# A softmax shift whose blockwise maxima reach one row through a TensorE transposition instead of a VectorE transposition and ScalarE copies

## The chip, the cores and the metric

The kernel runs on one NeuronCore of a Trainium2 chip. The metric is device time in microseconds of one execution; lower is better. The engines are TensorE (PE; its weight loads are PEld), VectorE (DVE), ScalarE (ACT), GpSimd (POOL) and SyncE (SP), which here issues all DMAs. Each engine takes its instructions in the order in which they stand and waits on semaphores for the others.

## What is computed

A cross-attention block in float32: x is 8 x 256 x 512, ctx is 8 x 256 x 512, with 16 heads of 32 columns and an MLP of 2048.

```
x1  = layer_norm(x, ln1_w, ln1_b)
q, k, v = x1 @ q_w + q_b, ctx @ k_w + k_b, ctx @ v_w + v_b      # split into 16 heads of 32
scores  = where(mask, q @ k^T / sqrt(32), smallest float)
attn    = softmax(scores, axis=-1)
hidden  = (attn @ v) @ cproj_w + cproj_b + x
y       = gelu(layer_norm(hidden, ln2_w, ln2_b) @ fc_w + fc_b) @ proj_w + proj_b
out     = hidden + y
```

## The kernel before, in words

The batch is done in two groups of four (g = 0, 1). All products with a weight matrix (k, q, v, the output projection o, and the MLP's fc and pd) are Strassen-Winograd products: `quad` (L848) makes seven products P1 to P7 of half-size blocks into PSUM banks X, Y and W, and VectorE or ScalarE adds them up (`t1`, `c11`, `c22`, `c21`, `c12`). The MLP applies the scheme twice, one inside the other. The sums of weight blocks that it needs are made early (`fw`, `pw`, L1080) and kept in DRAM.

Attention runs in 32 units, each of four heads and one batch element (`scores`, L1009). A unit is named by group, head group and batch element, so 012 is group 0, head group 1, batch element 2. For a unit the steps are:

- `s`: 16 matmuls in which TensorE is split by rows, one head in each quarter; keys lie on the 128 partitions, in two chunks kc, queries along the free axis.
- `ev`: ScalarE brings the eight pieces to SBUF with the mask added, into two buffers `pr`, one for each pair of heads.
- `mx` (L1022): for each pair, one VectorE reduction that transposes blocks of 32 x 32 takes the maximum over 32 keys. Its 128 x 64 result holds, for both chunks, maxima over quarters of the keys.
- `mt` (L1026), `mc` (L1029), `fold` (L1030): the eight partial maxima of a query have to be brought together. VectorE transposes the 128 x 64 block in squares of 32; ScalarE copies partitions 32 to 63, 64 to 95 and 96 to 127 beside partitions 0 to 31, in three instructions; one VectorE reduction over eight values leaves 32 x 32 maxima.
- `md`, `mm`: the 4 KB go to DRAM and come back as one row, spread over all 128 partitions (512 KB).
- `less` (L1048): the row is subtracted, on GpSimd in two instructions or on VectorE in one; `exp` (ScalarE).
- `av` (L1057): TensorE split by columns makes the sums of the exponentials (`ones`) and the products with v; VectorE inverts and scales (`r`, `att`).

Nothing of this order is left to a scheduler. `PROGRAM` (L124) is a list of all operations, written out by hand or by a planner; each engine's instructions stand in the order in which their names appear there, and a letter behind the colon chooses the engine (V VectorE, A ScalarE, G GpSimd). `PLACES` (L355) gives each buffer its slot. PSUM has eight banks, named W0 to W2 and C0 to C4 in before; a buffer of kind W (products) or C (scores, `av`, transpositions) lies in a bank of its own kind unless the table says otherwise. The scores of a unit need four banks.

At the end, group 1's last product `pd14` leaves its fourth product (`pd14_V`) turned, four pairs of transpositions (`ps_o`, L1312) bring the rest into the same shape, and VectorE adds residual and products into `ot`. Three stores of `ot` end the kernel; before them SyncE issues the stores of `tq` (`so1`, L1344), which are cut into pieces of 128 bytes.

Of the kernel before, what the change touches and what calls it, by code (L numbers as in the profile page):

```python
# [10 lines left out]
F32 = mybir.dt.float32  # L11
# [5 lines left out]
P = 128  # L17
# [26 lines left out]
class Order:  # L44
# [49 lines left out]
    def run(self):  # L94
# [20 lines left out]
        for o in order:  # L115
            for b in o.bufs:
                if b.slot is None and b.name in where:
                    w = where[b.name]
                    b.home = w[0] if not w[0].isdigit() else b.kind
                    b.slot = int(w.lstrip("WC"))  # L120
# [11 lines left out]
fw0s2:V fw1_10_1 xt0_5 k0_0_P6 fw0i6_3:V xt0_4 k0_1_t1:V fw0i6_1:G cb fw0i5_1:G v0_1_P3 k0_0_t2:V kws4:G fw0i1_4:V
k0_1_P6 stats_x0_30 fw0i1_3:G fw1i1_1:V stats_x0_00 fw0i6_2:G k0_0_P5 fw1i1_3:V k0_1_t2:A xt0_7 v0_0_t2:V fw1i1_2:G
fw0_01_1 stats_x0_10 fw1i1_4:G fcd0_1_True aggr_x0_30 k0_1_P5 fw1i4_1:V qw01 aggr_x0_00 stats_x0_01 fw1i4_2:G
fw1_01_0 fw0i6_4:V fcd0_6_False stats_x0_11 k0_1_P7 k0_1_t3:A fw1_01_1 aggr_x0_01 fw0i7_3:V k0_0_t3:A eps_x0_0
fcd0_7_False stats_x0_31 pow_x0_0 qw00 aggr_x0_31 k0_1_P3 fw1i4_4:G k0_1_c22 fcd0_7_True fw0i5_2:G aggr_x0_11
fcd0_5_False nb_x0_0 k0_0_c11 fw0i5_4:G norm_x0_01:A v0_0_P5 aggr_x0_10 k0_1_c11 fw0i2_1:G norm_x0_00:A fw1i4_3:V
k0_1_c12:A fw0i2_2:V k0_0_P7 eps_x0_1 eps_x0_3 fw0i5_3:V stats_x0_20 pow_x0_3 stats_x0_21 pow_x0_1 k0_0_P3 nb_x0_3
nb_x0_1 fw0i2_3:V norm_x0_31:A aggr_x0_20 aggr_x0_21 eps_x0_2 fw0i2_4:V norm_x0_10:A pow_x0_2 k0_0_c22 fcd0_2_True
k0_1_P4 v0_0_t3:V fw1i2_1:G fcd1_4_True k0_0_c12:A fcd0_6_True norm_x0_11:A nb_x0_2 fw0s4:V kd0_0_11 k0_0_P4  # L140
fcd1_1_True vws3:V norm_x0_20:A fcd0_3_False fw1i2_2:V fcd0_5_True norm_x0_21:A qws1:V turn_x0_10 norm_x0_30:A
fw1i2_4:G k0_0_c21 turn_x0_00 x0_10:A turn_x0_20 turn_x0_30 x0_20:A v0_0_P3 x0_30:V qws3:G xt1_2 cb1_02 x0_00:V
v0_1_c12:A fw0i3_1:V turn_x0_31 fw1i2_3:V turn_x0_11 fw0i3_2:V x0_31:A turn_x0_21 fw1s1:V turn_x0_01 q0_0_P1
x0_01:A qws2:G v0_0_c12:V fcd1_5_False x0_21:A k0_1_c21 fcd1_2_True fw1i5_3:G cb1_20 x0_11:A q0_0_P2 cb1_03
q0_0_t1:A x0t1:V q0_1_P1 fw0i3_3:V q0_0_c11 x0t2:V s000 fw0i3_4:V x0t3:V q0_0_P6 ev000_11 ev000_31 fw1s3:V xt1_3
ev000_10 ev000_01 cb1_12 q0_0_P7 x0t4:V kd0_0_21 q0_0_t2:A fcd1_7_False q0_1_t1:A fw1s2:V ev000_21 ev000_00 q0_0_P5
mx000_0 fw1s4:G fcd1_6_False cb1_10 q0_1_P6 q0_0_t3:A ev000_30 q0_0_c22 ev000_20 stats_x1_10 fcd1_3_False q0_1_P2
fw1i3_3:V fw1i5_1:V q0_1_t2:V fw1i5_2:G mx000_1 q0_0_P4 fw1i6_1:G qws4:G q0_1_c11 q0_1_P5 q0_0_c21 fw1i5_4:V mt000
fw0i4_3:G fcd1_5_True mc000_3 mc000_2 s020 cb1_13 mc000_1 fw1i6_3:G fold000 cb1_00 fw1i7_1:V q0_0_P3 md000 ev020_30
fw0i4_1:V ev020_21 fw1i7_2:V cb1_23 ev020_00 fw0i4_2:G cb1_21 ev020_10 fw1i7_4:G ev020_20 cb1_01 q0_1_P7 ev020_01  # L150
cb1_11 fw1i3_1:G ev020_31 q0_0_c12:A mx020_1 fw1i6_2:G ev020_11 s002 fw1i3_2:G mm000 mx020_0 fw0i4_4:G v0_1_P7
fw1i7_3:G mt020 stats_x1_11 mc020_2 mc020_3 fw1i6_4:G q0_1_t3:V ev002_30 ev002_11 fw1i3_4:G aggr_x1_10 aggr_x1_11
v0_0_P7 mc020_1 q0_1_c22 ev002_01 ev002_00 fold020 ev002_10 eps_x1_1 md020 ev002_31 pow_x1_1 ev002_20 q0_1_P3
# [358 lines left out]
def tile_xattn_block(  # L512
# [43 lines left out]
    def tile_of(b):  # L556
        if b.t is None:
# [874 lines left out]
    W = {}  # L1432
# [66 lines left out]
```

## Time and profile before

| | |
|---|---|
| three runs | 662.99, 663.53 (median) and 665.47 us |
| span of the profiled execution, first to last instruction | 662.0 us |
| own time of the profiled execution, beyond its span | not recorded apart; the runs lie 1.0 to 3.5 us above the span |
| instructions | 11469 |
| granted TensorE clock, mean over the span | 1.000 |
| DMA | 144.84 MB, mean 219 GB/s |

The profile is of one execution. A group line gives the line of the code, the engine, the operation, what it writes and reads, the shapes and the count, then busy time in us and the mean ns of one, then the engine's idle time just before and what ended it. A timeline line gives start and duration in us. Matmuls are pipelined, so the duration of one is longer than the step to the next one's start; the step is what it costs TensorE when it has no wait. For a DMA the issuing engine's instruction is shown, not the transfer.

### The profile page before, as it was taken

How to read it: one execution, taken by the hardware profiler on the slowest of the kernel's cores; microseconds unless marked ns; L12 is line 12 of the kernel's file. 1: busy time of each engine (PE TensorE's matmuls, PEld its weight loads, DVE VectorE, ACT ScalarE, POOL GpSimd, SP SyncE). 2: the span in 40 equal slices, each digit the busy share in tenths (PEclk: the TensorE clock that was granted, in tenths of full speed). 3: DMA queues.
4: the chain of work that ended last, by engine and by line, in shares of the span. 5: the costliest groups of instructions: out<-in, count | busy, mean ns of one | idle time of the engine just before them, and what ended most of it. 6: DMA issues, size and time to landing. Idle time of an engine off the chain costs nothing.

```text
span 662.0 us, 11469 instructions
## 1 busy us (share of the span) xinstructions
PE 654.6 (99%) x3925; PEld 490.0 (74%) x3925; DVE 585.7 (88%) x980; ACT 342.4 (52%) x702; POOL 374.8 (57%) x340
## 2 busy tenths in 40 slices
PE   8999999999999999999999999999999999999997
PEld 7746554477544776777688888888888888888887
DVE  2998799999999999999999998997789787998775
ACT  2046479799999899866995572030020013930000
POOL 1262773646888997699958774423535217720260
PEclk9999999999999999999999999999999999999999
DMA  8999888786574467886878698889978779359366
GB/s 250 311 356 307 211 197 291 267 255 125 144 241 161 144 202 234 263 268 197 266 249 273 198 235 225 289 269 230 195 193 241 190 201 242 93 142 240 106 141 111
DMA packets 206586, 144.84 MB, mean 219 GB/s; under 512 B 117008, under 2 KB 166976, under 8 KB 206528
## 3 DMA queue, kind: packets, MB, share of 16 engines
q1 hardware_dynamic: 206528, 144.11, 76.8%
q8 instruction: 31, 0.51, 0.3%
q14 instruction: 27, 0.22, 0.1%
HBM read 104.10 MB, written 39.98 MB: 218 GB/s over the span
## 4 chain that ended last, share of the span: by engine, by line
PE 92%; DVE 5%; ACT 1%; DMA 1%; issue 0%; SPq 0%; POOL 0%; DVEq 0%; ACTq 0%
PE pd_X L639 15%; PE fc_X L639 14%; PE fc_W L639 8%; PE av L639 7%; PE pd_W L639 7%; PE s L639 4%; PE o_X L639 4%; PE q_X L639 4%; PE k_X L639 4%; PE v_X L639 4%; PE pd_Y L639 4%; PE fc_Y L639 4%; PE q_W L639 2%; PE k_W L639 2%; PE v_W L639 2%; PE o_W L639 2%
## 5 line engine op out<-in xcount | busy, mean ns | idle before, releaser
L1047 POOL TENSOR_TENSOR pr<-pr,mm 128x512 f32<-128x512 f32 x84 | 110.4, 1346 | 22.8 <-DMA mm<-md 9.2
L619 ACT ACTIVATE pr<-s,cols 128x256 f32<-128x256 f32 x256 | 104.5, 482 | 21.8 <-PE s L639 15.8
L1022 DVE TRANSPOSE_TENSOR_REDUCE mx<-pr 128x32 f32<-128x1024 f32 x64 | 77.6, 1223 | 3.3 <-ACT pr L619 3.3
L1227 ACT ACTIVATE h<-h,cols 128x256 f32<-128x256 f32 x128 | 54.1, 498 | 36.7 <-DVE h L630 36.6
L1050 ACT ACTIVATE pr<-pr 128x1024 f32<-128x1024 f32 x64 | 66.9, 1069 | 3.4 <-POOL pr L1047 2.8
L630 DVE TENSOR_TENSOR h<-fc_X,h 128x512 f32<-128x512 f32 x80 | 52.8, 679 | 6.2 <-PE fc_X L639 5.5
L630 DVE TENSOR_TENSOR h<-fc_W,h 128x512 f32<-128x512 f32 x48 | 32.0, 679 | 5.8 <-PE fc_W L639 5.3
L639 PE MATMUL av<-pr,ones 128*32 128x256 f32 x512 | 34.2, 384 | 0.7 <-ACT pr L1050 0.6
L1029 ACT COPY mx<-mx 32x64 f32<-32x64 f32 x96 | 23.1, 243 | 19.8 <-DVE mx L1026 15.8
L1042 DVE TENSOR_TENSOR pr<-pr,mm 128x1024 f32<-128x1024 f32 x22 | 30.8, 1407 | 0.0
L628 POOL TENSOR_TENSOR z1i<-h,z1i 128x512 f32<-128x512 f32 x4 | 5.7, 1440 | 40.4 <-PE pd_X L639 40.4
L639 PEld LDWEIGHTS av<-pr,ones 128*32 128x32 f32 x512 | 14.1, 109 | 18.5 <-issue 6.7
L630 POOL TENSOR_TENSOR h<-h,fl 128x512 f32<-128x512 f32 x9 | 11.5, 1295 | 24.6 <-DVE fl L630 15.0
L639 PE MATMUL fc_W<-y1i,fl 128*128 128x256 f32 x100 | 24.6, 380 | 0.0
L639 PE MATMUL fc_X<-y1i,fl 128*128 128x256 f32 x88 | 21.6, 381 | 0.0
L639 PEld LDWEIGHTS fc_W<-y1i,fl 128*128 128x128 f32 x100 | 18.9, 190 | 2.9 <-DVE h L630 0.3
L639 PE MATMUL pd_W<-z0i,pl 128*128 128x256 f32 x88 | 20.6, 379 | 0.0
L1030 DVE TENSOR_REDUCE mx<-mx 32x32 f32<-32x256 f32 x32 | 18.4, 574 | 1.4 <-ACT mx L1029 1.3
L639 PE MATMUL pd_X<-z0i,pl 128*128 128x256 f32 x80 | 18.9, 379 | 0.0
L606 ACT COPY fl<-fc_X 128x512 f32<-128x512 f32 x6 | 3.5, 580 | 29.5 <-PE fc_X L639 29.2
L639 PEld LDWEIGHTS fc_X<-y1i,fl 128*128 128x128 f32 x88 | 16.6, 190 | 2.6 <-ACT h L606 0.2
L639 PEld LDWEIGHTS pd_W<-z0i,pl 128*128 128x128 f32 x88 | 16.7, 190 | 2.3
(595 smaller groups left out, 1815.6 us busy)
## 6 DMA issues: line engine op xcount, KB each, us to landing
mm<-md SPq DMA_DIRECT2D x32, 512.0 KB, 5.1
pl<-prd SPq DMA_DIRECT2D x47, 256.0 KB, 4.2
fl<-fcd SPq DMA_DIRECT2D x41, 256.0 KB, 4.0
fl<-prd SPq DMA_DIRECT2D x24, 256.0 KB, 3.8
fw<-in_L_xattn_fc_w_dram SPq DMA_DIRECT2D x16, 256.0 KB, 4.9
pw<-in_L_xattn_proj_w_dram SPq DMA_DIRECT2D x32, 128.0 KB, 3.6
hid<-in_x_dram SPq DMA_DIRECT2D x8, 512.0 KB, 4.8
hd<-hid SPq DMA_DIRECT2D x8, 512.0 KB, 3.4
```

The costliest lines, as they stand in the source:

```text
L606: (nc.scalar.copy if e == "ACT" else nc.vector.tensor_copy)(to(), of_())
L619: lambda e: nc.scalar.activation(to(), of_(), AF.Identity, bias=bias(), scale=1.0))
L628: nc.gpsimd.tensor_tensor(to()[:, ts(k, 512)], in0()[:, ts(k, 512)], in1()[:, ts(k, 512)], op)
L630: E[e].tensor_tensor(to(), in0(), in1(), op)
L639: nc.tensor.matmul(o(), l(), r(), start=first, stop=True, skip_group_check=True)
L1022: T.op(f"mx{u}_{h}", [("DVE", 1.126)], [(pr[h], None)], [(mx, [h])], lambda e, h=h: nc.vector.tensor_reduce(tile_of(mx)[:, 0:64].rearrange ...
L1029: lambda e, a=a: nc.scalar.copy(tile_of(mx)[0:32, 64 + 64 * a : 128 + 64 * a], tile_of(mx)[32 * a : 32 * a + 32, 64:128]))
L1030: T.op(f"fold{u}", [("DVE", 0.38)], [(mx, [2, 3, 4, 5])], [(mx, [6])], lambda e: nc.vector.tensor_reduce(tile_of(mx)[0:32, 320:352], tile_ ...
L1042: nc.vector.tensor_tensor(p_, p_, m_[:, :, None, :].to_broadcast([P, 2, 2, S]), ALU.subtract)
L1047: E[e].tensor_tensor(p_, p_, at(M, j)[:, None, :].to_broadcast([P, 2, S]), ALU.subtract)
L1050: lambda e, h=h: nc.scalar.activation(tile_of(pr[h]), tile_of(pr[h]), AF.Exp), table="exp")
L1227: lambda e, f=f, b=b, c=c: nc.scalar.activation(at(h[f][b], c), at(h[f][b], c), AF.Gelu_apprx_tanh, bias=col(c_fcb + f * 4 + c), scale=1.0 ...
```

## The change

`mt` and the three `mc` go. In their place come, for each unit:

- `km`: a VectorE maximum over the two key chunks, 128 x 64 to 128 x 32;
- `pt`: a TensorE transposition of the whole 128 x 96 (the maxima and km's result) into a PSUM bank `tm`, of which the last 32 rows are used;
- `fold`: a VectorE maximum over the four quarters, read from those 32 rows of PSUM.

`pr` is laid out with the key chunk outside and the head inside, so that `less` subtracts the same 512 values from both halves: on GpSimd without a broadcast. The buffer `mx` is 128 columns wide instead of 352. All eight PSUM banks are now one pool (`B0` to `B7`), each of which any product, score block or transposition may use. `PROGRAM` and `PLACES` are written anew from end to end: every engine's order is another one, and some additions go to another engine (for instance `z`, the sums of the MLP's activations: 20 on GpSimd before and 26 now; `pw`: 40 and 49; `out`: 3 and 8). The number of TensorE products is the same.

```diff
-SLOTS = {"Q": (45, 1024), "P": (36, 512), "H": (14, 256), "sm": (10, 32), "mx": (3, 352)}
-BANKS = {"W": 3, "C": 5}
+SLOTS = {"Q": (45, 1024), "P": (36, 512), "H": (14, 256), "sm": (10, 32), "mx": (3, 128)}
+BANKS = ("W", "C")
...
-vw10 c0_01:A turn_c0_20 mk c0_30:A c0t1:G c0_20:V v0_0_t1:A vw01 turn_c0_21 v0_1_t1:V turn_c0_31 fw0_11_1 k0_0_P2
...
-                b.t = banks.tile([P, 512], F32, tag=f"{b.home}{b.slot}", name=b.name)
+                b.t = banks.tile([P, 512], F32, tag=f"B{b.slot}", name=b.name)
...
-                copy(f"ev{u}_{j}{kc}", (pr[j // 2], [2 * (j % 2) + kc]), (sb[j], [kc]), lambda j=j, kc=kc: at(pr[j // 2], 2 * (j % 2) + kc),
+                copy(f"ev{u}_{j}{kc}", (pr[j // 2], [2 * kc + j % 2]), (sb[j], [kc]), lambda j=j, kc=kc: at(pr[j // 2], 2 * kc + j % 2),
                      lambda j=j, kc=kc: at(sb[j], kc), 256, lambda kc=kc: col(2 * (4 * g + b) + kc))
-        mx = Buf(f"mx{u}", "mx", 7)
+        mx = Buf(f"mx{u}", "mx", 4)
...
-                tile_of(mx)[:, 0:64].rearrange("p (k j q) -> p j k q", k=2, j=4)[:, 2 * h : 2 * h + 2],
+                tile_of(mx)[:, 0:64].rearrange("p (k j q) -> p k j q", k=2, j=4)[:, :, 2 * h : 2 * h + 2],
...
-        T.op(f"mt{u}", [("DVE", 0.15)], [(mx, [0, 1])], [(mx, [2])], lambda e: nc.vector.transpose(tile_of(mx)[:, 64:128], tile_of(mx)[:, 0:64]))
-        for a in range(1, 4):
-            T.op(f"mc{u}_{a}", [("ACT", 0.2)], [(mx, [2])], [(mx, [2 + a])],
-                 lambda e, a=a: nc.scalar.copy(tile_of(mx)[0:32, 64 + 64 * a : 128 + 64 * a], tile_of(mx)[32 * a : 32 * a + 32, 64:128]))
-        T.op(f"fold{u}", [("DVE", 0.38)], [(mx, [2, 3, 4, 5])], [(mx, [6])], lambda e: nc.vector.tensor_reduce(
-            tile_of(mx)[0:32, 320:352], tile_of(mx)[0:32, 64:320].rearrange("p (m c) -> p c m", c=32), axis=mybir.AxisListType.X, op=ALU.max))
+        T.op(f"km{u}", [("DVE", 0.13)], [(mx, [0, 1])], [(mx, [2])], lambda e: nc.vector.tensor_reduce(
+            tile_of(mx)[:, 64:96], tile_of(mx)[:, 0:64].rearrange("p (k n) -> p n k", k=2), axis=mybir.AxisListType.X, op=ALU.max))
+        tm = Buf(f"tm{u}", "C")
+        T.op(f"pt{u}", [("PE", 0.11)], [(mx, [0, 1, 2]), (ident, None)], [(tm, None)],
+             lambda e: nc.tensor.transpose(tile_of(tm)[0:96, 0:P], tile_of(mx)[:, 0:96], ident.t), mode="full")
+        T.op(f"fold{u}", [("DVE", 0.2)], [(tm, None)], [(mx, [3])], lambda e: nc.vector.tensor_reduce(
+            tile_of(mx)[64:96, 96:128], tile_of(tm)[64:96, 0:P].rearrange("p (a r) -> p r a", a=4), axis=mybir.AxisListType.X, op=ALU.max))
...
             def less(e, h=h):
+                m_ = at(M, 2 * h, 2)
                 if e == "DVE":
-                    p_ = tile_of(pr[h]).rearrange("p (i k q) -> p i k q", i=2, k=2)
-                    m_ = tile_of(M)[:, 512 * h : 512 * h + 512].rearrange("p (i q) -> p i q", i=2)
-                    nc.vector.tensor_tensor(p_, p_, m_[:, :, None, :].to_broadcast([P, 2, 2, S]), ALU.subtract)
+                    p_ = tile_of(pr[h]).rearrange("p (k n) -> p k n", k=2)
+                    nc.vector.tensor_tensor(p_, p_, m_[:, None, :].to_broadcast([P, 2, 512]), ALU.subtract)
                     return
-                for i in range(2):
-                    j = 2 * h + i
-                    p_ = at(pr[h], i, 1, 512).rearrange("p (k q) -> p k q", k=2)
-                    E[e].tensor_tensor(p_, p_, at(M, j)[:, None, :].to_broadcast([P, 2, S]), ALU.subtract)
+                for k in range(2):
+                    p_ = at(pr[h], k, 1, 512)
+                    E[e].tensor_tensor(p_, p_, m_, ALU.subtract)
```

Where an order is quoted in the prediction, a row is the line of the code, the operation, what it writes and reads, the shape, a count where equal rows follow one another, and in brackets the engines or DMA queues (DMAHW) for whose semaphores it waits. `k1_0_X` is the X bank of k's product for group 1, first half; `s012_0` the scores of unit 012, first head; `tm010` the bank of unit 010's transposition; `mx022` unit 022's maxima; `tq` and `ot` the last outputs.

More of the change, by code (lines that the diff above doesn't have):

```diff
@@ L117, in run @@
                 if b.slot is None and b.name in where:
-                    w = where[b.name]
-                    b.home = w[0] if not w[0].isdigit() else b.kind
-                    b.slot = int(w.lstrip("WC"))
+                    b.slot = int(where[b.name])
         return order
 PROGRAM = """
-cq0_00_1 cq0_00_0 vw00 cq0_01_1 cq0_01_0 rows8 rows7 cq0_10_0 turn_c0_00 rows0 turn_c0_10 c0_00:A cq0_10_1 c0_10:V
-cq0_11_0 small v0_0_P1 cq0_11_1 kw01 turn_c0_11 fw0_01_0 v0_1_P1 c0_11:A vw11 rows5 turn_c0_01 rows2 turn_c0_30
@@ L132 @@
[L132 to L141, printed above, removed]
@@ L646, in tile_xattn_block @@
     nc.vector.memset(warm, 1.0)
-    first = banks.tile([P, 512], F32, tag="W0", name="first")
+    first = banks.tile([P, 512], F32, tag="B0", name="first")
     def small(n):
@@ L1032, in scores @@
+        tm = Buf(f"tm{u}", "C")
[3 more added lines that the diff above has]
+            tile_of(mx)[64:96, 96:128], tile_of(tm)[64:96, 0:P].rearrange("p (a r) -> p r a", a=4), axis=mybir.AxisListType.X, op=ALU.max))
         md = dram(f"md{u}", [32, 32])
-        store(f"md{u}", md, None, [(mx, [6])], lambda: md.t, lambda: tile_of(mx)[:32, 320:352], 0.01)
+        store(f"md{u}", md, None, [(mx, [3])], lambda: md.t, lambda: tile_of(mx)[64:96, 96:128], 0.01)
```

660 lines of the change are left out of this document (331 added, 329 removed).

## Prediction

> **What bounds the kernel now.** I read the page's first part, then the chain that ended last.
>
> ```profile
> span 662.0 us, 11469 instructions
> PE 654.6 (99%) x3925; PEld 490.0 (74%) x3925; DVE 585.7 (88%) x980; ACT 342.4 (52%) x702; POOL 374.8 (57%) x340
> PE 92%; DVE 5%; ACT 1%; DMA 1%; issue 0%; SPq 0%; POOL 0%; DVEq 0%; ACTq 0%
> ```
>
> TensorE is busy for 654.6 of 662.0 us, and 92% of the chain lies on it. So the question is what the change does to TensorE's own work and to the few waits in it. The view of waits, for TensorE alone, and the windows around the longest of them:
>
> ```profile
> PE ps_y L726 <- DVE att L630: 1.2, 2, 1.0
> PE first L651 <- DVE warm L646: 1.0, 1, 1.0
> PE av L639 <- ACT pr L1050: 0.6, 1, 0.6
> PE v_X L639 <- DMA vw<-in_L_xattn_v_w_dram: 0.5, 1, 0.5
> PE fc_Y L639 <- DVE h L630: 0.2, 1, 0.2
> PE ps_c L726 <- DMA cq<-in_ctx_dram: 0.2, 1, 0.2
> 250.00:275.00 25.00, 23.50 (x264) 16.41 (x256) 24.18 (x55) 23.66 (x40) 16.71 (x19) 1.00 0.76 235
> 275.00:300.00 25.00, 24.34 (x167) 18.58 (x164) 24.48 (x40) 16.69 (x39) 23.50 (x25) 1.00 0.79 262
> 300.00:325.00 25.00, 25.00 (x228) 17.42 (x227) 23.57 (x44) 18.36 (x33) 23.38 (x23) 1.00 0.77 232
> ```
>
> Columns of the last three: length, then busy time of PE, PEld, DVE, ACT, POOL, the granted clock, and DMA. All of TensorE's waits come to 3.7 us; the first matmul's 1.0 stays in any order, which leaves 2.7 us that a better order could win. VectorE is nearly as full as TensorE in the attention stage (24.5 of 25 us), but TensorE does not wait for it there except where attention hands over to the MLP.
>
> The three runs give 662.99 to 665.47 us, median 663.53. The median is 1.5 us above the span; I put the profiled execution's own time at span plus 1.5. A difference of 0.5%, 3.3 us, is about what a measurement of this kernel can tell from none.
>
> **What the change takes away.** These rows are the steps that go or are replaced, 32 units each:
>
> ```profile
> L1026 DVE STREAM_TRANSPOSE mx<-mx 128x64 f32<-128x64 f32 x32 | 7.4, 234 | 0.6
> L1029 ACT COPY mx<-mx 32x64 f32<-32x64 f32 x96 | 23.1, 243 | 19.8 <-DVE mx L1026 15.8
> L1030 DVE TENSOR_REDUCE mx<-mx 32x32 f32<-32x256 f32 x32 | 18.4, 574 | 1.4 <-ACT mx L1029 1.3
> L1073 DVE TRANSPOSE_TENSOR_REDUCE rc<-av 128x8 f32<-128x256 f32 x32 | 13.6, 426 | 2.5 <-PE av L639 2.4
> ```
>
> ScalarE loses 23.1 us of copies. VectorE loses 234 + 574 = 808 ns a unit and gains km (64 elements in a partition; nearest row the transposition of as many, 234; half to double of that, I take 230) and the new fold, 128 elements from PSUM. Its bounds are half the old fold, 287, and the whole reduction of 256 elements from PSUM, 426; I take 350. That is 580 for 808, some 7 us less in all. None of this is on TensorE, so I cost both at nothing: what hides them is TensorE's own row of matmuls. The subtraction `less` has the same number of elements on either engine, and only its broadcast moves; nothing as well.
>
> **What it adds on TensorE.** Thirty-two transpositions. The nearest rows are the four-in-a-row transpositions of layer norm's output, here with the plain matmuls and one block of scores behind them in the timeline (start, duration):
>
> ```profile
> 50.38 0.27 PE L726 MATMUL ps_x<-ident,xn_x 128*128 128x128 f32 x1
> 50.49 0.27 PE L726 MATMUL ps_x<-ident,xt 128*128 128x128 f32 x1
> ...
> 52.01 0.27 PE L726 MATMUL ps_x<-ident,kws 128*128 128x128 f32 x1
> 52.12 1.89 PE L639 MATMUL v_X<-vws,c 128*128 128x256 f32 x8
> ...
> 57.32 1.88 PE L639 MATMUL q_Y<-x,qw 128*128 128x512 f32 x4
> 59.03 1.88 PE L639 MATMUL q_X<-x,qw 128*128 128x512 f32 x4
> 60.84 1.15 PE L639 MATMUL s<-q,xt 32*128 32x256 f32 x16
> 61.92 1.98 PE L639 MATMUL q_X<-x0t,xn_x 128*128 128x512 f32 x4
> 63.74 1.88 PE L639 MATMUL q_W<-x0t,kws 128*128 128x512 f32 x4
> ```
>
> A transposition shows 0.27 us, but the next one starts 0.11 after it, and the matmul behind the last one (52.01 to 52.12) also 0.11. So one costs 0.11 us of TensorE's time, and 32 cost 3.5 us. Charged at its whole duration, 0.27, it would be 8.6; that is taken up with the rivals.
>
> The same rows price a change of array shape. Four q matmuls take 1.71 (57.32 to 59.03), but 1.81 ahead of the scores and 1.82 behind them (61.92 to 63.74): 0.1 on each side, and about as much again inside the scores. Call it 0.2 a change. Counted in the two orders, TensorE changes between full, row (s) and column (av) shape 98 times before and 96 times now: 0.4 us less. A transposition keeps the full shape, so between full matmuls it changes nothing. But there is one lone, narrow transposition in the trace, and it is dear:
>
> ```profile
> 17.29 3.62 PE L639 MATMUL v_Y<-vw,c 128*128 128x256 f32 x16
> 20.74 1.88 PE L639 MATMUL k_X<-c,kw 128*128 128x512 f32 x4
> ...
> 24.19 1.88 PE L639 MATMUL k_X<-c,kw 128*128 128x512 f32 x4
> ...
> 26.00 0.27 PE L687 MATMUL ps_cols<-ident,rows 64*128 64x64 f32 x1
> 26.20 3.72 PE L639 MATMUL v_X<-vws,c0t 128*128 128x256 f32 x16
> 29.76 1.88 PE L639 MATMUL k_X<-c0t,kws 128*128 128x512 f32 x4
> ```
>
> It stretches the matmuls ahead by 0.10 (1.81 for 1.71), stands 0.20 itself, and stretches those behind by 0.11 (3.56 for 3.45): 0.4 us. It uses 64 rows of the array; the new one uses 128 rows and 96 columns. I take 0.11 because the shape 128 by 96 has the full height, and keep 0.4 for a rival. The Trainium skill's page "TensorEngine Tiling (Array Packing)", section "Tiling Modes", says that changing the mode drains TensorE, and lists 128, 64 and 32 columns, so that 96 belongs to the full mode; no row here shows 96.
>
> **The new waits.** Before, TensorE stood in no unit's chain from maximum to shift. Now it does. TensorE, at one place of the first attention group (unit 012's scores), before:
>
> ```order
> L639 MATMUL k1_0_X_954<-c1t2_1027,kws2_358 128x512 [waits DVE_49]
> L639 MATMUL k1_0_X_954<-c1t2_1027,kws2_358 128x512
> L639 MATMUL k1_1_X_969<-c1t2_1027,kws2_358 128x512 [waits Activation_49]
> L639 MATMUL k1_1_X_969<-c1t2_1027,kws2_358 128x512
> L639 MATMUL s012_0_1101<-q0_0_22_730,k0_1_12_521 128x256 [waits Activation_49]
> L639 MATMUL s012_1_1103<-q0_0_22_730,k0_1_12_521 128x256
> ```
>
> and now, with unit 010's transposition (tm010) ahead of the same scores:
>
> ```order
> L626 MATMUL k1_0_X_959<-c1t1_1000,kws1_312 128x512 [waits Activation_49]
> L626 MATMUL k1_0_X_959<-c1t1_1000,kws1_312 128x512
> L1017 MATMUL tm010_1125<-ident_64,mx010_1045 96x128 [waits DVE_49,Activation_49]
> L626 MATMUL s012_0_1129<-q0_1_12_902,k0_1_12_556 128x256
> L626 MATMUL s012_1_1131<-q0_1_12_902,k0_1_12_556 128x256 [waits DVE_49,PE_49]
> ```
>
> The transposition waits for VectorE's km and for ScalarE to clear the bank; queued behind it are the next scores, and behind those everything. On VectorE, around unit 022's maxima, before:
>
> ```order
> L1022 TENSOR_REDUCE mx022_918<-pr022_1_899 128x2x2x8 [waits DMAHW1_49,Activation_49]
> L1022 TENSOR_REDUCE mx022_918<-pr022_0_906 128x2x2x8 [waits Activation_49]
> L1026 STREAM_TRANSPOSE mx022_918<-mx022_918 128x64 [waits DVE_49]
> L630 TENSOR_TENSOR xt1_3_699<-q0_1_W_799,xt1_3_699 128x512 [waits PE_49]
> L630 TENSOR_TENSOR v0_0_21_456<-v0_0_W_849,v0_0_21_456 128x512
> L741 STREAM_TRANSPOSE c1_01_952<-cb1_0_613 128x512 [waits DMAHW2_49]
> L1030 TENSOR_REDUCE mx022_918<-mx022_918 32x32 [waits DVE_49,Activation_49]
> ```
>
> and now:
>
> ```order
> L1009 TENSOR_REDUCE mx022_944<-pr022_1_907 128x2x16 [waits Activation_49]
> L728 STREAM_TRANSPOSE c1_11_872<-cb1_2_910 128x512 [waits DMAHW4_49,DMAHW6_49,DMAHW2_49,DMAHW0_49]
> L1013 TENSOR_REDUCE mx022_944<-mx022_944 128x32 [waits DVE_49]
> L728 STREAM_TRANSPOSE c1_10_954<-cb1_2_910 128x512
> L1018 TENSOR_REDUCE mx022_944<-tm022_1004 32x32 [waits PE_49]
> ```
>
> A DMA wait on VectorE can now sit ahead of km, and so ahead of TensorE. In the new program 11 of the 32 transpositions have no TensorE operation written between their km and themselves. Each of the 11 can wait up to km plus the step from engine to engine: 0.23 + 0.20 (the last rows below: VectorE takes up pd_X at 655.94, 0.20 after TensorE has gone on at 655.74). That is 0 to 4.7 us; I take 2.0, since TensorE may run behind. Of the 2.7 us of old waits the new order closes some: I take 1.2, between 0 and 2.7.
>
> **The end.** The last steps before:
>
> ```profile
> L599 SPq DMA_DIRECT2D out_dram<-tq x16: 316/507/984, 640.9 to 654.9; - x16
> 655.74 1.11 PE L1312 MATMUL ps_o<-ident,po 128*128 128x128 f32 x8
> 655.94 0.42 DVE L630 TENSOR_TENSOR po<-pd_X,po 128x256 f32<-128x256 f32 x1 [0.97 <-PE pd_X L639]
> 656.69 1.95 PE L639 MATMUL pd_V<-fl,z1i 128*128 128x128 f32 x16
> 656.72 2.78 SPq L599 DMA_DIRECT2D out_dram<-ot  x3
> 658.68 0.42 DVE L630 TENSOR_TENSOR ot<-pd_V,ot 128x256 f32<-128x256 f32 x1 [0.99 <-PE pd_V L639]
> ```
>
> SyncE's last stores before:
>
> ```order
> L599 DMA out_dram<-tq_0_5594 32x32x32
> L599 DMA out_dram<-tq_1_5780 32x32x32 x4
> L599 DMA out_dram<-tq_0_5594 32x32x32
> L599 DMA out_dram<-ot_5839 128x2x128
> L599 DMA out_dram<-ot_5844 128x2x256
> L599 DMA out_dram<-ot_5839 128x2x128
> ```
>
> and now:
>
> ```order
> L586 DMA out_dram<-tq_1_5750 32x32x32 x3
> L586 DMA out_dram<-tq_2_5686 32x16x32
> L586 DMA out_dram<-ot_5808 128x2x128
> L586 DMA out_dram<-ot_5817 128x2x256
> L586 DMA out_dram<-tq_1_5750 32x32x32
> L586 DMA out_dram<-ot_5808 128x2x128
> ```
>
> A tq_1 store has moved in ahead of the last one, and three follow an addition that VectorE makes only after pd14's second product, so at about the time of 655.74. An issue takes 0.32 to 0.98 us. Four, two ot stores of about 0.4, and the late one come to 3 to 5.5 us; the last store was free to go 3.4 after that point (658.68 + 0.42). So it is 0 to 2 us late; I take 0.5.
>
> **The sum.** 663.5 + 3.5 (transpositions) - 0.4 (shape changes) + 2.0 (new waits) - 1.2 (old waits closed) + 0.5 (end) = 667.9, say 668.0.
>
> **The rivals.**
>
> 1. *The new order closes the old gaps and its waits are covered.* Then 663.5 + 3.5 - 0.4 - 2.7 = 663.9 at best; up to 666.8. It decides where km is done before TensorE arrives at all 32 places. For it: ScalarE and VectorE are 30 us lighter, and 1.8 of those 2.7 us lie where attention meets the MLP (ps_y and av). Against it: 32 more meeting points with an engine that is 24.5 us busy of 25. Faster than 660.2 would need TensorE's own work to shrink, and no row offers that.
> 2. *VectorE becomes the pacemaker of attention.* All 32 wait their 0.43, which is 13.8 us for the 2.0 of the sum, so 679.7; with half of each covered by the matmul ahead 6.9, so 672.8. Against it: VectorE's work falls by 7 us.
> 3. *A lone transposition is charged more than its spacing in a row of them*: its whole duration of 0.27, 8.6 for 3.5, so 673.0; or like ps_cols 0.4, 12.8 for 3.5, so 677.2. It decides from 0.2 us each on. For it: ps_cols is the only lone one in the trace. Against it: full height, neighbours of the same shape, and the 0.11 from the last of a row to the matmul behind it. The Trainium skill's page "TensorE: Matmul & The Clock Gate", section "Part 4: PE-mode transpose", gives about 275 ns for one in a kernel's context, which by itself would make 8.8 us, an estimate; the trace's duration agrees with it, the trace's spacing does not charge it.
>
> **How the numbers follow.** Forecast 0.45 (its own range 666.9 to 671), first rival 0.35, second 0.10, third 0.10. Not slower is the first rival, 0.35, of which 0.02 for faster by over 0.5%; the rest, 0.65, is slower. The range 664 to 675 leaves out the upper halves of the second and third rival and the lower rim of the first, together under 0.2.
>
> **What would show it.** In the new profile: 32 transpositions with 0.11 to the next start (0.4 would be rival 3); TensorE's waits by line, with tm on mx between 0 and 5 us; ScalarE about 23 us less busy; VectorE about 7 less; the last store issued 0 to 2 us later behind the last transpositions. TensorE busy falling below 655 would make the sum wrong at its root.

## The result and the profile after

Thirteen runs of the changed kernel, 667.44 to 674.84 us, have a median of 669.21 us; as many of the kernel before, on the same chip, 663.53. The ratio is 1.0079, with an interval of 1.0058 to 1.0099: slower by 0.8%. Timed twice more beside the kernel before (`e6_after_again`, `e11_after_beside` below) it gave 1.0051 (1.0024 to 1.0079) and 1.0089 (1.0052 to 1.0126). The profiled execution has a span of 665.4 us, 3.4 more than before. It is the fastest of the thirteen, and the medians lie 5.7 us apart, so 2.3 us of that difference stand in no trace. The page, first part and the shares of the chain:

```profile
span 665.4 us, 11434 instructions
PE 654.3 (98%) x3957; PEld 494.8 (74%) x3957; DVE 570.1 (86%) x956; ACT 312.9 (47%) x599; POOL 424.1 (64%) x378
PE 76%; DVE 9%; DMA 3%; POOL 2%; issue 1%; ACT 1%; SPq 0%; DVEq 0%; POOLq 0%; ACTq 0%
```

TensorE does 32 matmuls more and is busy for 0.3 us less. So the 3.4 us are not in its work. DMA, 1% of the chain before, now holds 3%. TensorE's own share of the chain has fallen from 92% to 76%, though it is as busy as before, so the chain alone doesn't say where the 3.4 us lie. The view of waits, TensorE alone:

```profile
PE first L638 <- DVE warm L633: 1.0, 1, 1.0
PE av L626 <- DVE hid L617: 0.8, 1, 0.8
PE v_X L626 <- DVE c L593: 0.8, 1, 0.8
PE av L626 <- DVE h L617: 0.7, 1, 0.7
PE q_X L626 <- DVE x L764: 0.4, 1, 0.4
PE q_X L626 <- DMA qw<-in_L_xattn_q_w_dram: 0.3, 1, 0.3
PE av L626 <- DVE att L617: 0.3, 1, 0.3
PE ps_c L713 <- DMA cq<-in_ctx_dram: 0.2, 1, 0.2
```

No row has `tm`: TensorE waits at none of its 32 new transpositions long enough to be listed. The old rows on `ps_y` and on `pr` are gone, others stand in their place, and the sum is 4.5 us for 3.7. The new steps' groups (operation, count; busy time and mean ns; idle time ahead of them) and two transpositions in the timeline:

```profile
L1018 DVE TENSOR_REDUCE mx<-tm 32x32 f32<-32x128 f32 x32 | 9.3, 289 | 4.6 <-PE tm L1017 3.7
L1013 DVE TENSOR_REDUCE mx<-mx 128x32 f32<-128x64 f32 x32 | 6.7, 211 | 0.6
```

```profile
331.33 1.03 PE L626 MATMUL fc_W<-y0i,kws 128*128 128x256 f32 x4
332.19 0.27 PE L1017 MATMUL tm<-ident,mx 128*96 128x128 f32 x1
332.30 1.03 PE L626 MATMUL fc_X<-y0t,kw 128*128 128x256 f32 x4
333.16 1.03 PE L626 MATMUL fc_X<-y0i,ow 128*128 128x256 f32 x4
```

The group ahead of the transposition takes 0.86 (331.33 to 332.19), as does the one behind it (332.30 to 333.16), and the transposition itself 0.11. From the start of a transposition to the next matmul it is 0.11 us in 18 of the 32 places, 0.15 in seven, 0.20 to 0.24 in the six that stand ahead of a change of shape, and 0.39 in one; together 4.7 us, where 32 times 0.11 are 3.5. It is VectorE that waits for TensorE's transpositions, 3.7 us in seven of them, and not the other way round.

Now the end, from the timeline. The columns are start, duration, engine, operation and count:

```profile
655.25 4.03 SPq L586 DMA_DIRECT2D out_dram<-tq  x5
656.04 1.12 PE L1299 MATMUL ps_o<-ident,po 128*128 128x128 f32 x8
657.00 1.95 PE L626 MATMUL pd_V<-fl,z1i 128*128 128x128 f32 x16
658.99 0.42 DVE L617 TENSOR_TENSOR ot<-pd_V,ot 128x256 f32<-128x256 f32 x1 [0.89 <-PE pd_V L626]
659.37 1.33 SPq L586 DMA_DIRECT2D out_dram<-ot  x2
660.75 0.49 SPq L586 DMA_DIRECT2D out_dram<-tq  x1
661.35 0.60 SPq L586 DMA_DIRECT2D out_dram<-ot  x1
```

TensorE begins its last product at 657.00, 0.31 later than before (656.69), and VectorE has the last tile ready at 659.41 (658.99 + 0.42). But its store is issued at 661.35, 1.9 us later; before, it was issued 0.03 us after VectorE. SyncE issues tq stores without a pause until 659.3, then the ot stores and the tq_1 store that moved in among them. The windows from 656 us on (length, busy time of PE, PEld, DVE, ACT and POOL, the granted clock, DMA share, GB/s), first after, then before:

```profile
656.00:659.00 3.00, 2.95 (x25) 2.61 (x23) 1.87 (x7) 0.00 (x0) 0.00 (x0) 1.00 0.95 144
659.00:662.00 3.00, 0.00 (x0) 0.00 (x0) 0.41 (x1) 0.00 (x0) 0.00 (x0) 0.88 0.96 199
662.00:665.40 3.40, 0.00 (x0) 0.00 (x0) 0.00 (x0) 0.00 (x0) 0.00 (x0) 0.50 0.47 98
```

```profile
656.00:659.00 3.00, 2.64 (x24) 2.35 (x21) 2.01 (x6) 0.00 (x0) 0.00 (x0) 1.00 0.78 162
659.00:662.00 3.00, 0.00 (x0) 0.00 (x0) 0.11 (x1) 0.00 (x0) 0.00 (x0) 0.93 0.30 95
```

After TensorE is done the DMA engines work on at 0.96 for three more microseconds; before, at 0.30.

I use two numbers for every kernel from here on. The **stretch** is the time from the first to the last start of a matmul; the last start is the last row's end less 0.27, which one matmul of that width shows. The **end** is from there to the span's end. Before: stretch 657.4, end 3.6. After: stretch 657.7, end 6.7. So 0.3 of the 3.4 us are TensorE's, 3.1 are behind it.

### The profile page after: what moved, and what is told of

Its sections match the earlier page's. It is cut to its first block, busy times and chain, and to the rows that moved or that the text cites. A ratio compares the mean times of both kernels' runs of the same rounds, so it can differ in the third digit from the quotient of the medians.

```text
span 665.4 us, 11434 instructions
## 1 busy us (share of the span) xinstructions
PE 654.3 (98%) x3957; PEld 494.8 (74%) x3957; DVE 570.1 (86%) x956; ACT 312.9 (47%) x599; POOL 424.1 (64%) x378
## 4 chain that ended last, share of the span: by engine, by line
PE 76%; DVE 9%; DMA 3%; POOL 2%; issue 1%; ACT 1%; SPq 0%; DVEq 0%; POOLq 0%; ACTq 0%
PE pd_X L626 15%; PE fc_X L626 13%; PE av L626 7%; PE fc_W L626 7%; PE pd_W L626 7%; PE q_X L626 4%; PE pd_Y L626 4%; PE fc_Y L626 3%; PE s L626 3%; PE o_X L626 3%; DVE mx L1009 3%; PE v_X L626 2%; PE v_W L626 2%; PE q_W L626 2%; DVE hid L617 1%
## 5 line engine op out<-in xcount | busy, mean ns | idle before, releaser
L606 ACT ACTIVATE pr<-s,cols 128x256 f32<-128x256 f32 x256 | 102.1, 486 | 53.5 <-PE s L626 40.3
L617 POOL TENSOR_TENSOR tq<-tq,rq 128x512 f32<-128x512 f32 x8 | 10.3, 1299 | 30.3 <-DVE tq L1326 13.8
L1030 DVE TENSOR_TENSOR pr<-pr,mm 128x1024 f32<-128x1024 f32 x21 | 25.2, 1213 | 1.4 <-DMA mm<-md 1.4
L626 PE MATMUL pd_X<-z0i,pl 128*128 128x256 f32 x104 | 24.4, 379 | 0.0
L626 PEld LDWEIGHTS pd_X<-z0i,pl 128*128 128x128 f32 x104 | 19.8, 190 | 2.7
L626 PE MATMUL fc_W<-y1i,fl 128*128 128x256 f32 x84 | 21.5, 380 | 0.0
L617 DVE TENSOR_TENSOR po<-pd_W,po 128x256 f32<-128x256 f32 x24 | 9.9, 414 | 10.0 <-PE pd_W L626 7.1
L615 POOL TENSOR_TENSOR z1i<-z1t,z1i 128x512 f32<-128x512 f32 x4 | 7.0, 1756 | 17.7 <-DVE z1t L617 17.7
L626 PEld LDWEIGHTS fc_W<-y1i,fl 128*128 128x128 f32 x84 | 15.9, 190 | 2.3 <-DVE fl L617 0.2
L1060 DVE TRANSPOSE_TENSOR_REDUCE rc<-av 128x8 f32<-128x256 f32 x32 | 14.1, 441 | 3.7 <-PE av L626 3.2
```

What stands on the lines that cost most here:

```text
L606: lambda e: nc.scalar.activation(to(), of_(), AF.Identity, bias=bias(), scale=1.0))
L615: nc.gpsimd.tensor_tensor(to()[:, ts(k, 512)], in0()[:, ts(k, 512)], in1()[:, ts(k, 512)], op)
L617: E[e].tensor_tensor(to(), in0(), in1(), op)
L626: nc.tensor.matmul(o(), l(), r(), start=first, stop=True, skip_group_check=True)
L1030: nc.vector.tensor_tensor(p_, p_, m_[:, None, :].to_broadcast([P, 2, 512]), ALU.subtract)
L1060: nc.vector.tensor_reduce(t, tile_of(av)[:, 256:512].rearrange("p (n r) -> p n r", r=32), axis=mybir.AxisListType.X, op=ALU.max, apply_tra ...
```

## The experiments

The theory I started from is the prediction's sum (called A in the first expectations): 0.11 us a transposition, some new waits, a late end. Its rivals were a transposition that costs more than its spacing (B), and an order whose worth hangs on the short way to the maxima (C). In the second batch the theory is called End. All kernels were timed in five rounds beside the kernel before.

| kernel | ratio to before, interval | stretch, us | end, us |
|---|---|---|---|
| `e1_twice` | 1.0083 (1.0050 to 1.0115) | 659.9 | 6.9 |
| `e2_new_order_old_reduction` | 1.0344 (1.0302 to 1.0386) | 675.0 | 7.0 |
| `e3_old_order_new_reduction` | 1.0118 (1.0080 to 1.0157) | 668.1 | 3.6 |
| `e4_no_tq1_stores` | 1.0003 (0.9978 to 1.0027) | 657.0 | 3.6 |
| `e5_old_no_tq1_stores` | 1.0027 (1.0001 to 1.0052) | 661.1 | 4.0 |
| `e6_after_again` | 1.0051 (1.0024 to 1.0079) | 657.4 | 7.5 |
| `e7_early_tail` | 1.0048 (1.0015 to 1.0082) | 660.2 | 3.6 |
| `e8_ot_first` | 1.0047 (1.0021 to 1.0072) | 658.8 | 7.5 |
| `e9_tail_b` | 1.0023 (0.9996 to 1.0051) | - | - |
| `e10_tail_c` | 1.0006 (0.9974 to 1.0038) | 658.4 | 4.7 |
| `e11_after_beside` | 1.0089 (1.0052 to 1.0126) | 657.8 | 6.8 |
| `e12_tail_c_beside` | 1.0032 (1.0009 to 1.0056) | 657.6 | 4.5 |

The profiled execution of `e9_tail_b` was one of its longest, 672.0 us, so its trace is left aside, and the end that was expected of it stays without a reading.

**Every transposition twice.** The price of a transposition, on its own.

```diff
-             lambda e: nc.tensor.transpose(tile_of(tm)[0:96, 0:P], tile_of(mx)[:, 0:96], ident.t), mode="full")
+             lambda e: [nc.tensor.transpose(tile_of(tm)[0:96, 0:P], tile_of(mx)[:, 0:96], ident.t) for _ in range(2)], mode="full")
```

> The kernel after, with every unit's transposition done twice into the same bank (32 more TensorE transpositions, nothing else moved). Theory A (a transposition costs TensorE its spacing, 0.11 us, and TensorE decides): 669.2 + 3.5 = 672.7 us, and the start of the last TensorE instruction 3 to 4 us later. Rival B (a lone transposition is charged its whole duration of 0.27 us or more, which the new order hid somewhere): 669.2 + 8.6 = 677.8 or more. Rival C (TensorE does not decide in the attention stage any more, VectorE or the end does): below 671.

The ratio, 1.0083, cannot be told from that of the changed kernel. In the trace the stretch is 2.2 us longer, for 32 transpositions:

```profile
L1032 PE MATMUL tm<-ident,mx x64: 272/273/316, 76.9 to 369.6; 128*96 128x128 f32 x64
PE 657.1 (98%) x3989; PEld 496.7 (74%) x3989; DVE 571.9 (86%) x956; ACT 312.9 (47%) x599; POOL 425.8 (64%) x378
```

Thirty-two spacings of 0.11 are 3.5 us, and TensorE's busy time grew by 2.8 (657.1 for 654.3). So in this trace one costs at most its spacing; that a part of the 32 fell into time in which TensorE would have waited anyway is likely, but not shown. The second of a pair follows the first at once, so this prices a transposition in a row; the price of a lone one is read from the timeline above. At 0.27 each the stretch would have grown by 8.6. B falls. The kernel before had a median of 665.79 us on this chip; the ratio on the 663.5 from which the theories reckon gives 669.0, which is below A's 672.7 too and within C's bound of 671. What C says of the order is for the next two.

**The new order with the old reduction.** `mt` stands in the place of km, the three ScalarE copies in that of the transposition, the fold where it is.

```diff
-        T.op(f"km{u}", ...
-        T.op(f"pt{u}", ...
+        T.op(f"mt{u}", [("DVE", 0.15)], [(mx, [0, 1])], [(mx, [2])], ...
+            T.op(f"mc{u}_{a}", [("ACT", 0.2)], [(mx, [2])], [(mx, [2 + a])], ...
...
-km000 ... pt000 ... fold000
+mt000 ... mc000_1 mc000_2 mc000_3 ... fold000
```

> The kernel after with its order and banks, but the reduction of before: where the VectorE maximum stood now stands the VectorE transposition, where the TensorE transposition stood now stand ScalarE's three copies, and the fold reads eight values from SBUF. Theory A (the transpositions cost TensorE 3.5 us, the new order itself saves TensorE some 3 us of stalls, and the end costs 2.2): 669.2 - 3.5 = 665.7, up to 667 where ScalarE's copies (23 us) come late. Rival B (the change's loss comes from meeting VectorE at 32 more places): 663 or less, since those waits go too. Rival C (the transposition shortens the way to the maxima and the order depends on it): 669 or more.

It is far slower than both, 1.0344. TensorE's two longest waits:

```profile
PE av L646 <- ACT pr L1056: 2.6, 3, 1.4
PE fc_X L646 <- DVE h L637: 2.4, 1, 2.4
```

The new order leaves no room for ScalarE's copies in the way from the maxima to the probabilities: `av` now waits for `pr`, which ScalarE writes, and the MLP's first products for tiles that VectorE has late. C holds, for the copies in these places; others weren't tried.

**The old order with the new reduction.** km in place of `mt`, the transposition in place of the last of the three copies, its bank chosen among those free there.

```diff
-mt000 ... mc000_3 mc000_2 ... mc000_1 ... fold000
+km000 ... pt000 ... fold000
```

> The kernel before with its order, only the reduction changed: VectorE maximum, TensorE transposition and VectorE maximum from PSUM in the places of the VectorE transposition, the copies and the fold, each in a PSUM bank that was free at that place; a few folds stand some places earlier because of that. Theory A: 663.5 + 3.5 = 667.0 where all waits are covered, up to 671 where a transposition waits for its bank or for VectorE; the end as before, with the last store issued 3.4 us after the turning transpositions begin. Rival B (the loss comes from the order laid out anew, not from the transposition): 663 to 664.

Slower by 1.2%. On the 663.5 from which the theories reckon that is 671.3 us, just over the upper edge of A's 667 to 671, and far from B's 663 to 664. TensorE's waits, three of them:

```profile
PE av L676 <- ACT pr L656: 1.9, 1, 1.9
PE s L676 <- DVE mx L1068: 1.1, 1, 1.1
PE tm L1067 <- DVE h L667: 0.6, 1, 0.6
```

The stretch grows by 10.7 us (668.1 for 657.4); the end stays at 3.6. Not all of the 10.7 is the reduction's. The longest row, on `pr`, waits for the copy `ev`, and the same wait stands at the same place in `e5_old_no_tq1_stores` below, which has the old order and the old reduction:

```profile
PE av L648 <- ACT pr L628: 1.7, 2, 1.5
```

Against that trace, with its stretch of 661.1, the growth is 7.0. Here the transpositions do cost what the prediction charged and more: 3.5 for themselves, and 3.4 in all the listed rows on `mx` and `tm`, of which two are above. So by the ratios the reduction alone loses at least about as much as the whole change (1.0118 for 1.0079, with intervals that overlap), the order alone loses far more, and the two together bring the stretch to within 0.3 us of before. How much better the old order would do with other banks for `tm` wasn't tried.

**Four stores left out, after and before.** The second block of 128 columns in the last 1024 rows of the output isn't written: the four stores of tq_1, 128 KB each, that the new order issues from 656.2 us on.

```diff
-                    for a in range(4):
+                    for a in range(4) if (g, c) != (1, 1) else ():
                         store(f"so{g}_{c}{a}", ...
```

> The kernel after without the four stores of tq_1, 128 KB each in pieces of 128 bytes: a quarter of the columns of group 1 of the output is not written. Theory A (the pieces crowd the last 12 us, back up SyncE, and the last store goes out 2.2 us late): the last store issues about 2 us sooner, 669.2 - 2.2 = 667.0, with the start of the last TensorE instruction unchanged. Rival B (the end is not limited by the stores but by the last addition): 669.

> The kernel before, with the same four stores of tq_1 (4 x 128 KB) left unwritten: the control to the kernel after without them. Theory End (the new order begins these stores too late, so they stand in front of the last store of ot): the kernel before issues them by 655.7 us and its last store, at 659.1, waits for VectorE alone, so little is won: ratio 0.997 to 1.000, last store issued 658.5 to 659.2. Rival Any (half a megabyte fewer stores is worth about 5 us in whatever kernel): ratio 0.990 to 0.994, and the run without stores of the kernel after then says nothing of the order.

The changed kernel without them is as fast as the kernel before, 1.0003, and its end is the old one, 3.6. On the 663.5 from which the theories reckon that is 663.7 us, below both A's 667.0 and B's 669: the four stores cost more than the 2.2 us of late issue that A had counted.

```profile
656.33 1.95 PE L640 MATMUL pd_V<-fl,z1i 128*128 128x128 f32 x16
656.80 2.35 SPq L600 DMA_DIRECT2D out_dram<-ot  x3
658.32 0.42 DVE L631 TENSOR_TENSOR ot<-pd_V,ot 128x256 f32<-128x256 f32 x1 [0.89 <-PE pd_V L640]
```

The kernel before gains nothing from leaving out the same four: 1.0027, even a little over the 1.000 that was expected at most, with an end of 4.0. So it is not the bytes that cost, but where the new order has them. The rival Any falls. This trace's stretch is 3.7 us over that of the other trace of the old order (661.1 for 657.4), in part by waits in attention, hundreds of microseconds ahead of the stores that are missing. So the stretch of a single trace can be off by that much; the ends differ by 0.4.

**The changed kernel again**, twice, to see how far single ratios are to be trusted; the kernel is word for word the changed one.

> The changed kernel once more, beside the others on one chip. All theories: ratio 1.006 to 1.010. Theory End: last TensorE start within 0.5 us of 658.7 in a profile of 665 to 666 us, last store issued 661 to 662. A ratio outside 1.004 to 1.012 would say that single ratios of this study are not to be trusted to half a per cent.

> The changed kernel beside tail C on one chip, since the two have been timed only on different chips so far. Theory End: 1.005 to 1.009, 2 to 4 us over tail C. Rival (tail C's 1.0006 was a better chip, not a better end): within 1 us of tail C.

The ratios 1.0051 and 1.0089 lie on both sides of the first, and the first is below the 1.006 expected; stretch (657.4 and 657.8) and end (7.5 and 6.8) repeat well. For this kernel the trace's two numbers are the steadier measure. The kernel before has a single trace, so the 0.3 us by which the stretches differ is no better known than that one.

**The ot stores issued first.** Is it the order of SyncE's issues, or what the DMA engines still have to move?

```diff
-out1_11:V so1_13 so1_12 so1_11 turn_o10 ... so1_21 st00 ot01 st1 pd14_P4 so1_10 oz st01
+out1_11:V turn_o10 ... so1_21 st00 ot01 st1 pd14_P4 oz st01 so1_13 so1_12 so1_11 so1_10
```

> The changed kernel with the four stores of tq_1 issued behind the three of ot, nothing else moved. Theory End in its narrow form (SyncE's order: the ot stores stand behind four slow issues): the three ot stores are issued at 657.5 to 659.6, but the tq_1 stores then follow, and the end moves by less than 1 us either way: ratio 1.006 to 1.010. If only the last store of ot were what counts, the ratio would fall to 1.003 to 1.005. Rival Drain: no change, or later by up to 3 us, since the pieces of 128 bytes now run last: ratio 1.008 to 1.013.

```profile
658.55 2.35 SPq L601 DMA_DIRECT2D out_dram<-ot  x3
660.07 0.42 DVE L632 TENSOR_TENSOR ot<-pd_V,ot 128x256 f32<-128x256 f32 x1 [0.89 <-PE pd_V L641]
660.99 2.86 SPq L601 DMA_DIRECT2D out_dram<-tq  x4
```

Now the ot stores go as soon as VectorE has written (the last at 660.5, later than expected, in a trace whose stretch is 1.4 us longer than that of the changed kernel in the same batch), and the four of tq_1 follow from 660.99. The end is 7.5, no better than the 7.5 of the changed kernel in the same batch. The ratio, 1.0047, by itself would fit the case in which the last ot store alone counts, 1.003 to 1.005; but the changed kernel had 1.0051 in this batch, so nothing was won. An unmoved end was among the outcomes of the narrow form and of Drain alike, so the run doesn't part these two. It speaks against the last ot store alone: which store goes first made no difference here, since the same bytes are still to be moved when TensorE is done.

**An earlier tail.** All work is kept; only the last 25 us are in another order, so that the tq_1 stores can begin earlier. With the products move their loads, the transpositions and sums behind them and the stores, and one sum of tq_1 (`out1_10`) goes from GpSimd to VectorE. In the changed kernel the products pd14_P7, P6 and P5 stand between or ahead of pd13_P4 and pd12_P4, on which tq_1 waits.

```diff
-pd14_P7 pd13_P5 ... pd13_P7 ... pd14_P6 ... pd13_P3 ... pd12_P3 ... pd14_t2 pd14_P5 ... pd13_P4 ... pd12_P4 ... pd14_P2 ... pd14_P3
+pd13_P5 ... pd13_P7 ... pd14_P6 ... pd13_P3 ... pd12_P3 ... pd13_P4 ... pd12_P4 pd14_t2 pd14_P5 pd14_P7 ... pd14_P2 ... pd14_P3
```

> The changed kernel with all its work, only its last 25 us in another order: pd13_P4 and pd12_P4 ahead of pd14_P5 and pd14_P7, their loads and the transpositions and sums of tq_1 behind them at once, the stores sorted by when their tile is done. Theory End: the four stores of tq_1 begin 3 to 4 us earlier (652 to 653 for 656.2), the last store of ot is issued at 658.8 to 659.8, the ratio falls to 1.000 to 1.005. Rival Drain (what ends the span is the sum of bytes behind some moment, whichever come first): last store at 660.5 or later, ratio 1.006 or more. Rival Any: ratio unchanged, 1.006 to 1.010.

```profile
659.52 1.95 PE L641 MATMUL pd_V<-fl,z1i 128*128 128x128 f32 x16
659.98 2.35 SPq L601 DMA_DIRECT2D out_dram<-ot  x3
661.51 0.42 DVE L632 TENSOR_TENSOR ot<-pd_V,ot 128x256 f32<-128x256 f32 x1 [0.90 <-PE pd_V L641]
```

The end is repaired in full, 3.6 us, where Drain would have left it as it was. The tq_1 stores begin at 654.9 and the last ot store is issued at 662.0, both later than expected, because TensorE itself is 2.5 us later in this trace (last start 661.2 for 658.7); seen from there, the tq_1 stores begin 6.3 us ahead for 2.5. A new row stands in TensorE's waits, made by my order: pd13_P5 now comes right behind pd13_P6, with which it shares its bank, and waits until VectorE has emptied it.

```profile
PE pd_X L641 <- DVE po L866: 1.2, 1, 1.2
```

The stretch is 660.2, 2.8 us over that of the changed kernel in the same batch (657.4). The new row is 1.2 of them; most of the rest are listed waits far ahead of what was moved (`q_X` on `qw` 0.6, `s` on `att` 0.6, `q_X` on `x` 0.4). The ratio, 1.0048, lies in End's 1.000 to 1.005, but so near the changed kernel's 1.0051 that this run alone doesn't settle it; two more layouts of the tail were made for that.

**Two tails without that wait.** Tail B puts pd14_P2 between pd13_P6 and pd13_P5; tail C leaves pd14_P7 there and moves pd14_P5 alone of the products. Loads, sums and stores are laid out much as in the early tail, and tail B gives pd14's Y another bank.

```diff
 tail B
-pd14_P7 pd13_P5 ... pd14_P5 ... pd13_P4 ... pd12_P4 ... pd14_P2 ... pd14_P3
+pd14_P2 pd13_P5 ... pd13_P4 ... pd12_P4 pd14_t2 pd14_P5 pd14_P7 ... pd14_P3
 tail C
-pd14_P7 pd13_P5 ... pd14_P5 ... pd13_P4 ... pd12_P4 ... pd14_P2 ... pd14_P3
+pd14_P7 pd13_P5 ... pd13_P4 ... pd12_P4 pd14_t2 pd14_P5 ... pd14_P2 ... pd14_P3
```

> The changed kernel with all its work, the last 25 us laid out once more: pd13_P4 and pd12_P4 ahead of pd14_P5 and pd14_P7 as in the early tail, but pd14_P2 now stands between pd13_P6 and pd13_P5, so that TensorE has no 1.2 us wait there, and VectorE brings pd14_t3 ahead of the last sum of tq_1. Theory End: nothing of the tail is behind SyncE, so the span ends 3.5 to 3.7 us behind the last TensorE start (6.7 to 7.5 in the changed kernel, 3.6 in the kernel before), TensorE's busy stretch is that of the changed kernel (657.0 to 657.9 from first to last start), the granted clock of its runs is back at 0.999 to 1.000, and the ratio is 1.000 to 1.003. Rival: the changed kernel has a loss that does not stand at the end (the early tail won only 1.2 us of 3): ratio 1.004 or more though the end is repaired.

> The same with one product less moved: pd14_P7 stays where the changed kernel has it, pd14_P5 alone goes behind pd13_P4 and pd12_P4, so the stores of tq_1 gain 1.7 us instead of 3.4. Theory End: still enough for the last store to wait for VectorE alone or for at most 0.7 us of SyncE: end 3.6 to 4.4 us behind the last TensorE start, ratio 1.000 to 1.004. Rival: as for the other tail, 1.004 or more.

> Tail C beside the changed kernel. Theory End: 1.000 to 1.004, 2 to 4 us under the changed kernel, end 4 to 5 us behind the last TensorE start. Rival: within 1 us of the changed kernel.

1.0023 and 1.0006, both inside what End expected (tail C's first end, 4.7, is a little over its 4.4); and beside the changed kernel on one chip, tail C's median is 666.59 us for 670.32, 3.7 less, at ratios of 1.0032 and 1.0089. The trace of that run of tail C:

```profile
656.92 1.95 PE L641 MATMUL pd_V<-fl,z1i 128*128 128x128 f32 x16
657.93 2.15 SPq L601 DMA_DIRECT2D out_dram<-ot  x3
658.91 0.42 DVE L632 TENSOR_TENSOR ot<-pd_V,ot 128x256 f32<-128x256 f32 x1 [0.89 <-PE pd_V L641]
659.00:662.00 3.00, 0.00 (x0) 0.00 (x0) 0.34 (x1) 0.00 (x0) 0.00 (x0) 0.93 0.76 204
```

The last store is issued 0.3 us behind VectorE, the DMA engines are at 0.76 after 659 for 0.96, and the end is 4.5, with the stretch as in the changed kernel. With the two kernels that leave the stores out, this shows the cause: of the changed kernel's loss, most is the late start of tq_1's stores. Moving one product behind two others, with the loads, sums and stores that go with it, takes two thirds of the loss away (3.7 of 670.32 less 664.81, the kernel before there). How much of that is the product's place and how much the order of the stores behind it wasn't tried apart. The trace puts 2.3 us of end on it (6.8 less 4.5), the medians 3.7; where the other 1.4 lie, in runs that have no trace, stays open. Tail C beats the changed kernel; against the kernel before it is even at best, 1.0006, and the second time a little slower, 1.0032 (1.0009 to 1.0056).

## Why the prediction was right or wrong

The number was right, 668.0 us for 669.21, in its range and on the likelier side. The sum behind it was not, and that the number came out was luck. The prediction named its own test: TensorE busy below 655 us would make the sum wrong at its root, and it is 654.3. That threshold was badly set, since the page before already had 654.6; what the sum asked for was a TensorE that is busy about 3 us longer, and it is busy 0.3 us less. The sum put 3.9 us on TensorE and 0.5 on the end; the traces show 0.3 and 3.1. One was 3.6 us too high and the other 2.6 too low.

- *Transpositions, 3.5.* Right. The spacing is 0.11 in the timeline, lone and with 96 columns, in 18 of 32 places (the other 14, with a change of shape or a short gap behind them, come to 1.2 us more), and doubling them adds no more than 0.11 each. This refutes the third rival. The 275 ns that the Trainium skill gives for one in a kernel's context (page "TensorE: Matmul & The Clock Gate", section "Part 4: PE-mode transpose") are what the row shows as its duration, 0.27; they are not what the kernel pays for it.
- *Shape changes, -0.4.* Not measured by itself. That a transposition keeps the full shape is borne out: the groups of matmuls on both sides of it keep their 0.86. The page "TensorEngine Tiling (Array Packing)" of the Trainium skill, section "Tiling Modes", lists modes of 128, 64 and 32 columns and none of 96, which agrees with this.
- *New waits, 2.0.* Too much: TensorE has no listed wait on `tm`. The bound of 0 was the right end. VectorE waits for the transpositions instead, 3.7 us, and no listed wait of TensorE follows from that.
- *Old waits closed, -1.2.* The rows with `ps_y` and `pr`, 1.8 us, are gone, but others came, and the listed waits rose from 3.7 to 4.5. What the order did close is not in the view of waits at all. Here is a stretch of the MLP before, and the same kind of stretch after:

```profile
528.12 1.03 PE L639 MATMUL fc_Y<-y1t,fl 128*128 128x256 f32 x4
528.99 1.03 PE L639 MATMUL fc_X<-y1i,fl 128*128 128x256 f32 x4
529.85 1.03 PE L639 MATMUL fc_W<-y1i,fl 128*128 128x256 f32 x4
530.80 1.13 PE L639 MATMUL fc_X<-y1t,fl 128*128 128x256 f32 x4
531.77 0.59 PE L639 MATMUL fc_W<-y1i,fl 128*128 128x256 f32 x2
```

```profile
529.91 1.03 PE L626 MATMUL fc_W<-y1i,fl 128*128 128x256 f32 x4
530.77 1.03 PE L626 MATMUL fc_X<-y1i,fl 128*128 128x256 f32 x4
531.64 1.03 PE L626 MATMUL fc_X<-y1t,fl 128*128 128x256 f32 x4
```

  After, each group of four follows the last by 0.86 (529.91, 530.77, 531.64). Before, the group at 530.80 comes 0.95 after the one ahead of it, and the next 0.97 after that: 0.19 us lost, with no wait in any row, since the matmuls' shown durations overlap the gap. Summed over all neighbours of full shape, as start to start less the usual spacing (0.216 us for 256 columns, 0.429 for 512, 0.109 for 128), and counting what lies above it, such losses come to 11.1 us before and 7.8 after. Listed waits are 2.0 in each, so 9.1 and 5.8 us stand in no row. The two other traces of the changed kernel have 5.9 and 6.1, and the kernel before without its four stores 10.2. Those 3.3 us paid for most of the transpositions; what makes the gaps isn't shown. I had counted as winnable only the 2.7 us that the view of waits lists. This is the first term that failed, and the first rival's mechanism: the new order closes old gaps and its own waits are covered. That rival forecast 663.9 to 666.8; its best value had no term for the end at all.
- *The end, 0.5 between 0 and 2.* The mechanism was named rightly (tq_1 stores behind VectorE's late sum, one in front of the last), the size was not: 3.1 us in the trace. I had added up SyncE's issues, and those give the 1.9 us by which the last store is late, inside the bound. What I left out is that the DMA engines are then at 0.95 of their time, so the last store also lands later: from its issue to the span's end it is 4.0 us for 2.8 before.
- *VectorE and ScalarE, at nothing.* Right. km and fold take 211 + 289 = 500 ns for the old 808, 9.9 us in all where I had put 7; VectorE fell by 15.6 and ScalarE by 29.5, where its copies were 23.1, since the new order also sends other work elsewhere (GpSimd is busy for 49.3 us more). The second rival falls with it. The nothing holds for this pair of kernels alone: in `e2_new_order_old_reduction` the new order with the old steps loses 3.4%, so the new order lives on the shorter way to the maxima.

The forecast of the sign rested on the wrong step, then: had the end been as I put it, the kernel would have been within 0.5% of the kernel before, as the tails and the run without the four stores show.

## What to carry to other kernels

When a whole order is laid out anew, compare the place of each large store with the end of the last engine: stores that are issued late are still being moved when the engines are done, and here that took the end from 3.6 us to 6.7. And when the pacing engine is 99% busy, look at the spacing of its instructions and not only at its listed waits: in the kernel before, gaps of 0.05 to 0.15 us came to 8.4 us, and all the waits of the view to 3.7.

## What the runs showed of the hardware

- A lone fp32 transposition of 128 rows by 96 columns delayed the full-shape matmuls behind it by 0.11 us in most places (0.15 in seven, 0.39 in one), as one in a row of them does, though its row shows 0.27.
- Stores of 32 x 32 x 32 and 32 x 16 x 32 elements, in runs of 32 floats, filled 0.95 of the DMA engines' time at 144 GB/s; with the ot stores among them, in runs of 128 or 256 floats, 0.96 at 199. One issue of such a store took SyncE between 0.32 and 0.90 us, the longest (at 658.4) with the engines at 0.92 from 658 to 659 us, and one of the shortest (at 651.2) with them at 0.00 from 651 to 652; in the changed kernel's second trace one took 1.86:

```profile
L586 SPq DMA_DIRECT2D out_dram<-tq x17: 316/557/902, 645.7 to 660.8; - x17
```

  The Trainium skill's page "DMA: Bandwidth & Descriptors", section "Specifications", gives 512 bytes as the least transfer for the full rate; a run of 32 floats is 128 bytes, and the trace agrees in direction (144 GB/s with such runs alone, 199 with longer ones among them).
- The granted clock falls behind TensorE's last matmul: 0.88 on average from 659 to 662 us, 0.50 from there on. These 6.4 us lose 0.12 x 3.0 + 0.50 x 3.4 = 2.1 us of clock, which is the 0.003 of 665.4 by which the mean of the changed kernel's span, 0.997, falls short. So the mean, 1.000 before, is the mark of its longer idle end, and no slower TensorE.
